# The last query block's norm and transposes as small steps inside the next scans or the last filter stage, and the start values of y inside the attention

## The chip, the cores and the metric

The kernel runs on one core of one Trainium2 chip. Its engines each work through their own queue in order: TensorE (PE; its weight loads are PEld), VectorE (DVE), ScalarE (ACT), GpSimd (POOL) and SyncE, whose queue (SPq) issues the transfers that matter here. The metric is the device time of one execution in microseconds (us); smaller is better.

## The reference

All data are float32. The input `x` has four images of 48 by 48 positions with 128 channels; the kernel treats them one after the other (b = 0 to 3), with L = 2304 positions (tokens) each. Two layers are computed.

```python
# layer 0: group norm, then a state-space block
x = x + _L0_conv_ref(_gn(x), ...)      # projection, 3x3 depthwise convolution, 4 directional scans:
    # h = h * exp(dt * A) + (dt * u) * B;  y = sum over states of h * C;  y += Ds * u
    # norm of y, gate by silu(z), projection back to 128 channels
# layer 1: attention, then a spectral filter block ("STU")
t = _to_tokens(x)
t = t + _L1_attn_ref(_ln_t(t))         # softmax(x x^T) x over all 2304 tokens, x normed per token
t = t + _L1_ffn_ref(_ln_t(t), ...)     # per-token norm to u; causal convolutions of u with 16 filters,
    # with u and with sign-alternating u, each followed by a 128x128 matrix; plus u at 3 lags
```

What this case concerns is `_ln_t(t)` between the attention and the STU: each of the 2304 tokens loses its mean over 128 channels and is divided by the root of its variance plus 1e-5. The result u is needed in two layouts, tokens by channels and (transposed) channels by tokens.

## The kernel before, in words

**Stages.** For each image there is first a scan stage (`scans`, L554), in which the scans of image b are woven with the STU of image b - 1 (`stu`, L957), and for image 0 with a preparation of matrices (`mixture`). Then comes an attention stage: `epilogue(b)` and `attention(b)` woven with `prologue(b + 1)` and `begin_scans(b + 1)`. After image 3 its STU runs alone (`stu_alone`, L1195). So there are four places where an attention stage ends: three times into a scan stage, once into the STU that runs alone. There is no planner: the order of the instructions of every engine is the order in which the generators of L1211 to L1265 emit them. Tile pools opened and closed with the stages set the buffers: a tile of a new stage waits for the last use of whatever lay in its memory.

**Scans.** The 24 chunks of an image (4 directions by 6 pieces of 384 positions) give 192 units of 8 per chunk. For one unit, DVE or POOL multiplies dt*u by the row of B (L481), ACT makes four decays exp(dt*A) (L490), DVE runs four scans (L497), POOL multiplies by C (L506), PE sums over states into y (L514), and DVE adds y to `ya` every fourth unit (L526). The decays and the copied rows of B (L473) lie in a `Ring` (L319) of four PSUM banks (five for image 0), whose first instruction is a DVE memset (L325). Other work may borrow a bank: `mm_hold` takes one, `mm_tile` gives its tile, `mm_done` returns it. `more` (called four times in every step of `scans`) advances the STU beside them.

**STU.** A matmul of filter rows (`tt`, fetched at L1010) with u and with `us`, the sums of two u's (L1051); evictions by ACT (L1067 to L1075); a matrix `G` (L1021) applied at L1114. The output rows are treated in five blocks of up to 126 rows; only the fourth and fifth block read `u[:, 3]`. At the start of each block `begin` fetches the transposed u from DRAM (`ud`, L1082 and L1083).

**Attention and its tail.** Queries are treated in five pieces in the order 0, 4, 1, 2, 3. For every piece 18 slots each make scores (L774), their exponential (L776) and the product with the values (L767). After a piece, `tail(b, J, ...)` (L910) does in steps, one per slot: copy the product (L917), transpose (L921), divide and add to T (L924 to L932), store T to `td` in DRAM (L934), read it back in another token order (`tu`, L937), norm it with `normed` (L149 to L158, with one square on ACT, L152, and one power on POOL, L156), form `us` (L943), transpose on PE (L947), copy to SBUF (L950), store to `ud` (L952). The tails of pieces 0, 4, 1 and 2 run beside the slots of later pieces. Piece 3 is the last, so L785 to L787 run its whole tail when no slot is left.

**Start values of y.** `start_y` (L305) writes Ds*u to `ya` (L309, two DVE instructions). It is called when `begin_scans` has given its last piece, which is at the last slot of the attention, ahead of the tail of piece 3 on DVE.

Of the kernel before, what the change touches and what calls it, by code (L numbers as in the profile page):

```python
# [8 lines left out]
F32 = mybir.dt.float32  # L9
# [6 lines left out]
P = 128  # L16
# [39 lines left out]
def hybrid_kernel(ctx: ExitStack, tc: tile.TileContext, a: dict, out: bass.AP):  # L56
# [262 lines left out]
    class Ring:  # L319


        def __init__(self, pool, n, name):
            self.t = [pool.tile([P, 512], F32, tag=f"ring{i}", name=f"{name}_{i}") for i in range(n)]
            for t in self.t:
                nc.vector.memset(t[:, 0:CS + 2:CS + 1], 0.0)  # L325
            self.free = list(range(n))
            self.held = []

        def take(self):
            return self.free.pop(0)  # L330
# [17 lines left out]
    def mm_done():  # L348
        if isinstance(bank["mm"], Ring):
            bank["mm"].free.append(bank["mm"].held.pop(0))  # L350

    class Chunk:

# [12 lines left out]
        def prep(self, pool):  # L366

            k, name, xc = self.k, self.name, xcs[self.b]
            xdd_ = xdd[k % 2][self.lo // CS]

            def rest(n=1):

                yield
                yield 0
                yield
                for i in range(3 * n - 3):  # L380
                    yield 0 if i % 3 == 1 else None

            if k >= 2:
                xd = self.xd = pool.xd.tile([P, CS], F32, tag="xd", name=f"xd{name}")
                nc.sync.dma_start(xd, xdd_)
            yield from rest(2)
            if k < 2:
                mm_hold()
            yield
            if k < 2:  # L390
                xd = self.xd = pool.xd.tile([P, CS], F32, tag="xd", name=f"xd{name}")
                ps = mm_tile(f"xp{name}")
                for h in range(NH):
                    nc.tensor.matmul(ps[:, :CS], xw[:, h, k, :], in_order(xc[h], k, self.lo, CS),
                                     start=(h == 0), stop=(h == NH - 1))
            yield 2 * CS if k < 2 else 0
            yield
            if k < 2:
                nc.scalar.activation(xd, ps[:, :CS], AF.Identity, bias=onerow)
                mm_done()  # L400
            yield from rest()

            re = pool.one.tile([P, NH, 2, CS], F32, tag="re", name=f"re{name}")
            for h in range(NH):
                mm_hold()
                yield
                ps = mm_tile(f"dt{name}_{h}")
# [4 lines left out]
                mm_done()  # L412
# [36 lines left out]
            yield 0  # L449
            load(1)  # L450
            yield
# [99 lines left out]
            next(preps[2])  # L551
        yield chunks, preps

    def scans(b, chunks, preps, front, sp, back, ring, work, work_cols):  # L554
# [60 lines left out]
        for s in range(len(units) + 2):  # L615
            real = s < len(units)
            enter(s)
            prepare(s)
            if real:
                scan(s, 0)  # L620
            more((s + 0.25) / len(units))
            if 1 <= s <= len(units):
                units[s - 1].times_c()
            if real:
                scan(s, 1)
            if pending:
                pending.pop().add_y()
            prepare(s)
            more((s + 0.5) / len(units))
            spread(s + 2)  # L630
            if real:
                scan(s, 2)
            more((s + 0.75) / len(units))
            prepare(s)
# [9 lines left out]
            more((s + 1) / len(units))  # L644
        for u in pending:
            u.add_y()
        assert next(work, None) is None
# [101 lines left out]
    def attention(b, T, xn, xnT, pool, tmp, ps):  # L749

        pieces = [0, 4, 1, 2, 3]
        slots = [(J, i) for J in pieces for i in range(NT)]
        es, po, tails = [], {}, []  # L760

        def values():
            J, i, e = es.pop(0)
            w = P * PIECES[J]
            if i == 0:
                po[J] = ps.two.tile([P, 512], F32, tag="o", name=f"o{b}_{J}")
            nc.tensor.matmul(po[J][:, :w], xn[:, i], e[:, :w], start=(i == 0), stop=(i == NT - 1))  # L767
# [139 lines left out]
        for t in us[b]:  # L907
            nc.gpsimd.memset(t[KP[-1]:, NM - 1], 0.0)

    def tail(b, J, T, po, pool, ps):  # L910


        u, sums = us[b]
# [18 lines left out]
        nc.vector.tensor_tensor(T[:, :, C - 1], T[:, :, C - 1], s, ALU.subtract)  # L932
        yield
        nc.sync.dma_start(tokens(td, J), T)  # L934
        yield
        x = pool.one.tile([P, 4, C], F32, tag="tu", name=f"tu{b}_{J}")
        nc.sync.dma_start(x[:k], td[512 * J:512 * J + 4 * k].rearrange("(p j) c -> p j c", j=4))  # L937
# [273 lines left out]
    for b in range(B):  # L1211
# [2 lines left out]
        ring = bank["mm"] = Ring(ps.psa, 4 if b else 5, f"ring{b}")  # L1214
        if b == 0:
            mixed = Stage(tc, "m", "right", two=(2, SB))
            scans(b, *first, front, sp, ps, ring, mixture(mixed, ps), MIX_COLS)
# [102 lines left out]
```

## Time and profile before

The median of three runs is 5857.22 us (5853.99 to 5860.59).

| what | value |
|---|---|
| profiled execution, its own time | 5857.79 us |
| its span | 5856.1 us |
| busy share of the span: PE, DVE, ACT, POOL | 84%, 73%, 57%, 62% |
| scan stages | about 110 to 1090, 1361 to 2382, 2643 to 3665, 3934 to 4932 us |
| STU alone | about 5171 us to the end |
| DVE scans L497 | 3072 instructions, 2702.4 us |
| PE filter matmuls L1051 | 818.0 + 811.8 + 797.0 us in the three largest groups |

The span is what the profile covers; the 1.7 us between it and the execution's own time lie before and after it. Busy shares are averages over stages with different limits, so the places where stages meet have to be read in the timeline, which lists the instructions of all engines in order of time: start, duration, engine, line, operation, tiles, and in square brackets how long the engine had been idle and which work ended that. Durations of PE are modelled.

### The profile page before, as it was taken

How to read it: one execution, taken by the hardware profiler on the slowest of the kernel's cores; microseconds unless marked ns; L12 is line 12 of the kernel's file. 1: busy time of each engine (PE TensorE's matmuls, PEld its weight loads, DVE VectorE, ACT ScalarE, POOL GpSimd, SP SyncE). 2: the span in 40 equal slices, each digit the busy share in tenths (PEclk: the TensorE clock that was granted, in tenths of full speed). 3: DMA queues.
4: the chain of work that ended last, by engine and by line, in shares of the span. 5: the costliest groups of instructions: out<-in, count | busy, mean ns of one | idle time of the engine just before them, and what ended most of it. 6: DMA issues, size and time to landing. Idle time of an engine off the chain costs nothing. (4 is left out here: it accounts for less than half of the span.)

```text
span 5856.1 us, 74080 instructions
## 1 busy us (share of the span) xinstructions
PE 4937.2 (84%) x23922; PEld 3149.3 (54%) x23922; DVE 4267.9 (73%) x4883; ACT 3333.3 (57%) x6957; POOL 3622.6 (62%) x1823
## 2 busy tenths in 40 slices
PE   3566555697999998788999998779999998889999
PEld 1211111344666667445566666436566666468889
DVE  6999999657999998548999997548999997200000
ACT  2777777346777776247777775247777764332111
POOL 1999999505889998207889997108898986000000
PEclk6777787798999999899999999889999999999999
DMA  3444454116878777127777787027877775045546
GB/s 107 162 161 162 160 168 158 56 48 190 240 250 258 249 254 265 43 70 216 231 252 251 250 266 240 21 89 223 243 251 257 248 261 188 14 116 158 158 146 209
DMA packets 750563, 1066.86 MB, mean 182 GB/s; under 512 B 158528, under 2 KB 561088, under 8 KB 750144
## 3 DMA queue, kind: packets, MB, share of 16 engines
q1 hardware_dynamic: 744352, 1058.83, 57.2%
q10 hardware_dynamic: 5824, 3.30, 0.3%
q8 instruction: 191, 3.13, 0.2%
q14 instruction: 196, 1.61, 0.1%
HBM read 943.80 MB, written 117.98 MB: 181 GB/s over the span
## 5 line engine op out<-in xcount | busy, mean ns | idle before, releaser
L497 DVE TENSOR_TENSOR_SCAN s<-ring,s 128x385 f32<-128x385 f32 x3072 | 2702.4, 938 | 123.3 <-ACT ring L490 121.9
L506 POOL TENSOR_TENSOR s<-s,bc 128x1536 f32<-128x1536 f32 x768 | 2440.0, 3179 | 128.5 <-DVE s L497 73.3
L490 ACT ACTIVATE ring<-rep,A 128x384 f32<-128x384 f32 x3072 | 1759.3, 584 | 778.6 <-DVE s L481 456.8
L481 POOL TENSOR_TENSOR s<-rep,bc 128x1536 f32<-128x1536 f32 x288 | 994.4, 3453 | 131.2 <-DMA bc<-xdd 124.2
L481 DVE TENSOR_TENSOR s<-rep,ring 128x1536 f32<-128x1536 f32 x480 | 831.4, 1733 | 86.6 <-ACT ring L473 36.5
L1051 PE MATMUL cx<-tt,us 128*128 128x254 f32 (+7 forms) x3840 | 818.0, 355 | 74.0 <-ACT U L1075 46.9
L514 PE MATMUL y<-s,csum 128*32 128x384 f32 x6144 | 718.1, 542 | 191.7 <-POOL s L506 119.5
L1051 PE MATMUL cx<-tt,u 128*128 128x254 f32 (+7 forms) x3840 | 811.8, 354 | 67.3 <-ACT cy L1067 67.2
L1051 PE MATMUL cy<-tt,u 128*128 128x252 f32 (+5 forms) x3840 | 797.0, 351 | 30.3 <-DMA tt<-fd 30.3
L1051 PEld LDWEIGHTS cx<-tt,u 128*128 128x128 f32 x3840 | 644.8, 192 | 312.6 <-issue 113.3
L1051 PEld LDWEIGHTS cx<-tt,us 128*128 128x128 f32 x3840 | 645.3, 193 | 275.2 <-issue 91.2
L1051 PEld LDWEIGHTS cy<-tt,u 128*128 128x128 f32 x3840 | 648.9, 193 | 178.0 <-issue 117.9
L1114 PE MATMUL pr<-U,G 128*128 128x288 f32 (+6 forms) x2048 | 590.5, 420 | 15.4 <-DMA G<-gd 15.1
L1141 DVE TENSOR_TENSOR res<-res,ot 126x512 f32<-126x512 f32 (+1 forms) x20 | 13.4, 672 | 686.8 <-PE ot L1135 686.8
L1114 PEld LDWEIGHTS pr<-U,G 128*128 128x128 f32 x2048 | 340.6, 191 | 169.4 <-issue 96.2
L514 PEld LDWEIGHTS y<-s,csum 128*32 128x32 f32 x6144 | 126.8, 112 | 551.0 <-issue 283.2
L776 ACT ACTIVATE e<-s,shift 128x512 f32<-128x512 f32 (+1 forms) x360 | 231.1, 644 | 328.5 <-PE s L774 327.9
L156 POOL TENSOR_TENSOR ln_vu<-ln_vu,mhalf 128x4 f32<-128x4 f32 (+1 forms) x20 | 21.8, 1092 | 625.5 <-DVE ln_vu L155 625.5
L774 PE MATMUL s<-xnT 128*128 128x512 f32 (+1 forms) x720 | 355.2, 578 | 45.7 <-ACT xnT L736 23.3
L894 PE MATMUL G<-M,W 128*128 128x256 f32 (+3 forms) x512 | 233.2, 571 | 189.1 <-ACT W L884 80.3
L767 PE MATMUL o<-e,xn 128*128 128x512 f32 (+1 forms) x720 | 341.6, 557 | 4.5 <-ACT e L776 4.5
L1074 ACT COPY U<-cx 128x252 f32<-128x252 f32 (+1 forms) x320 | 111.6, 349 | 400.8 <-PE cx L1051 398.4
(170 smaller groups left out, 4110.7 us busy)
## 6 DMA issues: line engine op xcount, KB each, us to landing
rep<-dtdud SPq DMA_DIRECT2D x768, 384.0 KB
bc<-xdd SPq DMA_DIRECT2D x3072, 48.0 KB
tt<-fd SPq DMA_DIRECT2D x192, 577.0 KB
tt<-fd SPq DMA_DIRECT2D x192, 505.0 KB
dtdud<-re SPq DMA_DIRECT2D x192, 384.0 KB
tt<-fd SPq DMA_DIRECT2D x192, 379.0 KB
G<-gd SPq DMA_DIRECT2D x192, 256.0 KB
tt<-fd SPq DMA_DIRECT2D x64, 506.0 KB
```

What stands on the lines that cost most here:

```text
L481: eng.tensor_tensor(s, self.ch.rep[self.h][:, :, 1], bt.unsqueeze(1).to_broadcast([P, G4, CS]), ALU.mult)
L490: nc.scalar.activation(ring.body(self.dA[g]), ch.rep[self.h][:, g, 0], AF.Exp, scale=A[:, ch.k, self.h * G4 + g, self.q:self.q + 1])
L497: nc.vector.tensor_tensor_scan(s, ring.decays(i, ch.rev), s, 0.0, ALU.mult, ALU.add)
L506: nc.gpsimd.tensor_tensor(self.s, self.s, ch.bc[Q4 + self.q].unsqueeze(1).to_broadcast([P, G4, CS]), ALU.mult)
L514: nc.tensor.matmul(ch.y[g * DL:(g + 1) * DL, :CS], csum, self.s[:, g], start=(self.q == 0), stop=(self.q == Q4 - 1))
L767: nc.tensor.matmul(po[J][:, :w], xn[:, i], e[:, :w], start=(i == 0), stop=(i == NT - 1))
L774: nc.tensor.matmul(p[:, :w], xnT[:, i * P:(i + 1) * P], xnT[:, 512 * J:512 * J + w], start=True, stop=True)
L776: nc.scalar.activation(e[:, :w], p[:, :w], AF.Exp, bias=shift)
L894: nc.tensor.matmul(p[:, :n], W[:, q if t else 0, i], M[t][:, i].unsqueeze(1).to_broadcast([P, n, C]), start=(t == 0 and i == 0), stop=(t = ...
L1051: nc.tensor.matmul(p4[:, 1:3, v - (hi - at):] if g else p4[:, 0:4:3, v - (hi - at):], x, t[:, :, hi - 1 - at + J * P:end if end >= 0 else ...
L1074: nc.scalar.copy(U[n][:, 2:8:5], p[:, :4 * (w + 1)].rearrange("p (e m) -> p e m", e=4)[:, 0:4:3, 1:])
L1114: nc.tensor.matmul(o if q else o.rearrange("p f r m -> p r f m"), G, U[n][:, 4 * q:4 * q + 4, v0:v1].rearrange("p (a b) m -> p a b m", a=2 ...
```

## The change

Three things change.

1. The tail of the last piece (J = 3) returns after storing T to `td` (L934). The read back, the norm, the sums, the transposes and the store to `ud` move to a new generator `finish(b)`, which the scan stage of the next image advances four times in every step, and which the STU that runs alone advances once at each of its yields. The norm is written with other instructions: `bn_stats` and `bn_aggr` on DVE instead of two reductions, a subtraction, a square and a product; the power and one small product on POOL; the scaling by four ACT instructions; the sums `us` by two PE matmuls with the identity, copied by ACT. Its PSUM comes from the ring, of which it borrows one bank at a time, twice. The STU that runs alone gets a ring of two banks for it. The small tiles `fin`, `fst` and `fmv` are new in the pool `keep`.
2. `start_y(b + 1)` is called before `begin_scans(b + 1)`, 25 slots before the attention's end instead of at its last slot.
3. `mm_hold` returns the bank that it took, and `mm_tile` and `mm_done` are given it, so that two borrowers can hold banks at the same time. For `prep` this leaves the order as it was.

```diff
@@ Ring, mm_hold, mm_tile, mm_done
     def mm_hold():
-        if isinstance(bank["mm"], Ring):
-            bank["mm"].held.append(bank["mm"].take())
-
-    def mm_tile(name):
-        if isinstance(bank["mm"], Ring):
-            return bank["mm"].body(bank["mm"].held[0])
+        return bank["mm"].take() if isinstance(bank["mm"], Ring) else None
+
+    def mm_tile(name, hold=None):
+        if hold is not None:
+            return bank["mm"].body(hold)
...
@@ scans: next(finish, None) behind each of the four more(...) of a step
             more((s + 0.25) / len(units))
+            next(finish, None)
...
@@ attention
-                tails.append(tail(b, J, T, po.pop(J), tmp, ps))
+                tails.append(tail(b, J, T, po.pop(J), tmp, ps, J == pieces[-1]))
@@ new
+    LAST = 3
+
+    def finish(b):
+        u, sums = us[b]
+        x = keep.tile([P, 4, C], F32, tag="fin", name=f"fin{b}")
+        st = keep.tile([P, 4, 6], F32, tag="fst", name=f"fst{b}")
+        mv = keep.tile([P, 4, 4], F32, tag="fmv", name=f"fmv{b}")
+        yield
+        nc.sync.dma_start(x, td[512 * LAST:512 * LAST + 4 * P].rearrange("(p j) c -> p j c", j=4))
+        for i in range(7):
+            yield
+        for j in range(4):
+            nc.vector.bn_stats(st[:, j], x[:, j])
+        for j in range(4):
+            nc.vector.bn_aggr(mv[:, j, 0:2], st[:, j:j + 1])
+        nc.vector.tensor_scalar_add(mv[:, :, 1], mv[:, :, 1], 1e-5)
+        nc.vector.tensor_scalar_mul(mv[:, :, 0], mv[:, :, 0], -1.0)
+        yield
+        nc.gpsimd.tensor_tensor(mv[:, :, 2], mv[:, :, 1], mhalf[:, :4], ALU.pow)
+        nc.gpsimd.tensor_tensor(mv[:, :, 3], mv[:, :, 0], mv[:, :, 2], ALU.mult)
+        for i in range(7):
+            yield
+        for j in range(4):
+            nc.scalar.activation(u[:, LAST, j], x[:, j], AF.Identity, bias=mv[:, j, 3:4], scale=mv[:, j, 2:3])
+        for i in range(4):
+            yield
+        for n in range(2):
+            hold = mm_hold()
+            p = mm_tile(f"fin{b}_{n}", hold)
+            for i, j in enumerate(range(4)[3 * n:3 * n + 3]):
+                nc.tensor.transpose(p[:, i * P:(i + 1) * P], u[:, LAST, j], ident)
+            if n:
+                for i in range(2):
+                    nc.tensor.matmul(p[:, P:3 * P], ident, u[:, LAST, 2 * i:2 * i + 2].rearrange("p j c -> p (j c)"),
+                                     start=(i == 0), stop=(i == 1))
+            yield
+            yield
+            if n:
+                nc.scalar.copy(x[:, 3], p[:, :P])
+                nc.scalar.copy(sums[:, LAST].rearrange("p j c -> p (j c)"), p[:, P:3 * P])
+            else:
+                nc.scalar.copy(x[:, :3].rearrange("p j c -> p (j c)"), p[:, :3 * P])
+            mm_done(hold)
+            yield
+            yield
+        nc.sync.dma_start(ud[:, :, 1 + P * LAST:1 + P * (LAST + 1)], x)
@@ tail
         nc.sync.dma_start(tokens(td, J), T)
+        if last:
+            return
         yield
@@ the stages
-            scans(b, *first, front, sp, ps, ring, stu_alone(b - 1, ps, 1), STU_COLS)
+            scans(b, *first, front, sp, ps, ring, finish(b - 1), stu_alone(b - 1, ps, 1), STU_COLS)
...
             front = Stage(tc, f"f{b + 1}", "left", one=(1, SB), xd=(3, SB), rep=(3, SB))
+            start_y(b + 1)
             pieces = begin_scans(b + 1, front)
...
-                if first:
-                    start_y(b + 1)
...
-    ps = Stage(tc, "end", "right", psc=(2, PSUM), psp=(1, PSUM))
+    ps = Stage(tc, "end", "right", psa=(1, PSUM), psc=(2, PSUM), psp=(1, PSUM))
+    bank["mm"] = Ring(ps.psa, 2, "ringe")
+    end = finish(B - 1)
     for _ in stu_alone(B - 1, ps, 2):
+        next(end, None)
+    for _ in end:
         pass
```

More of the change, by code (lines that the diff above doesn't have):

```diff
@@ L326, in __init__ @@
             self.free = list(range(n))
-            self.held = []
         def take(self):
@@ L338, in mm_hold, with mm_done @@
     def mm_hold():
-        if isinstance(bank["mm"], Ring):
-            bank["mm"].held.append(bank["mm"].take())
-    def mm_tile(name):
-        if isinstance(bank["mm"], Ring):
-            return bank["mm"].body(bank["mm"].held[0])
+        return bank["mm"].take() if isinstance(bank["mm"], Ring) else None
+    def mm_tile(name, hold=None):
+        if hold is not None:
+            return bank["mm"].body(hold)
         pool, tag = bank["mm"]
         return pool.tile([P, 512], F32, tag=tag, name=name)
-    def mm_done():
-        if isinstance(bank["mm"], Ring):
-            bank["mm"].free.append(bank["mm"].held.pop(0))
+    def mm_done(hold):
+        if hold is not None:
+            bank["mm"].free.append(hold)
     class Chunk:
@@ L387, in prep @@
             if k < 2:
-                mm_hold()
+                hold = mm_hold()
             yield
@@ L391, in prep @@
                 xd = self.xd = pool.xd.tile([P, CS], F32, tag="xd", name=f"xd{name}")
-                ps = mm_tile(f"xp{name}")
+                ps = mm_tile(f"xp{name}", hold)
                 for h in range(NH):
@@ L399, in prep @@
                 nc.scalar.activation(xd, ps[:, :CS], AF.Identity, bias=onerow)
-                mm_done()
+                mm_done(hold)
             yield from rest()
@@ L404, in prep @@
             for h in range(NH):
-                mm_hold()
+                hold = mm_hold()
                 yield
-                ps = mm_tile(f"dt{name}_{h}")
+                ps = mm_tile(f"dt{name}_{h}", hold)
                 nc.tensor.matmul(ps[:, :CS], dtw[:, k, h * P:(h + 1) * P], xd, start=True, stop=True)
@@ L411, in prep @@
                 nc.scalar.copy(re[:, h, 0], ps[:, :CS])
-                mm_done()
+                mm_done(hold)
                 if h == 0:
@@ L552, in begin_scans, with scans @@
         yield chunks, preps
-    def scans(b, chunks, preps, front, sp, back, ring, work, work_cols):
+    def scans(b, chunks, preps, front, sp, back, ring, finish, work, work_cols):
         units = [Unit(ch, h, q) for ch in chunks for h, q in quads]
@@ L629, in scans @@
             more((s + 0.5) / len(units))
+            next(finish, None)
             spread(s + 2)
@@ L633, in scans @@
             more((s + 0.75) / len(units))
+            next(finish, None)
             prepare(s)
@@ L644, in scans @@
             more((s + 1) / len(units))
+            next(finish, None)
         for u in pending:
@@ L908, in begin_stu, with tail @@
             nc.gpsimd.memset(t[KP[-1]:, NM - 1], 0.0)
-    def tail(b, J, T, po, pool, ps):
+    LAST = 3
[24 more added lines that the diff above has]
+        for n in range(2):
+            hold = mm_hold()
+            p = mm_tile(f"fin{b}_{n}", hold)
[12 more added lines that the diff above has]
+                nc.scalar.copy(x[:, :3].rearrange("p j c -> p (j c)"), p[:, :3 * P])
+            mm_done(hold)
+            yield
+            yield
+        nc.sync.dma_start(ud[:, :, 1 + P * LAST:1 + P * (LAST + 1)], x)
+    def tail(b, J, T, po, pool, ps, last):
         u, sums = us[b]
@@ L1216, in hybrid_kernel @@
             mixed = Stage(tc, "m", "right", two=(2, SB))
-            scans(b, *first, front, sp, ps, ring, mixture(mixed, ps), MIX_COLS)
+            scans(b, *first, front, sp, ps, ring, iter(()), mixture(mixed, ps), MIX_COLS)
             mixed.close()
         else:
-            scans(b, *first, front, sp, ps, ring, stu_alone(b - 1, ps, 1), STU_COLS)
+            scans(b, *first, front, sp, ps, ring, finish(b - 1), stu_alone(b - 1, ps, 1), STU_COLS)
         ps.close()
```

## The prediction

> **What bounds the kernel now.** I first read the busy time of each engine stage by stage. The columns are the stretch, then busy time and (instructions) of PE, PEld, DVE, ACT, POOL, then PE's clock and the DMA share.
>
> ```profile
> 1335.00:1361.00 26.00, 7.62 (x20) 3.25 (x18) 13.28 (x25) 6.21 (x9) 4.39 (x2) 0.64 0.18 57
> ...
> 1461.00:2380.00 919.00, 860.22 (x4818) 581.77 (x4818) 855.14 (x918) 636.62 (x1365) 808.71 (x391) 0.98 0.78 248
> ...
> 5155.00:5178.00 23.00, 5.65 (x15) 2.38 (x13) 6.39 (x17) 1.22 (x2) 1.01 (x1) 0.57 0.26 62
> ```
>
> Inside a scan stage DVE (93%) and PE (94%) set the pace together. Between the stages there are holes of over 20 us in which every engine is at half load or less. There are four. What fills such a hole is read in the timeline (start, duration, engine, line, operation); this is the one before the fourth scan stage:
>
> ```profile
> 3912.18 2.74 DVE L309 TENSOR_SCALAR ya<-xc,dsum 128x2304 f32<-128x2304 f32 x2
> ...
> 3914.84 0.68 DVE L917 COPY oT<-o 128x512 f32<-128x512 f32 x1
> ...
> 3918.72 0.16 DVE L932 TENSOR_TENSOR T<-T,den 128x4 f32<-128x4 f32 x1
> 3918.90 0.38 SPq L934 DMA_DIRECT2D td<-T  x1
> 3921.21 0.33 SPq L937 DMA_DIRECT2D tu<-td  x1
> 3923.85 0.69 DVE L149 TENSOR_REDUCE ln_su<-tu 128x4 f32<-128x512 f32 x1 [4.97 <-DMA tu<-td]
> ...
> 3928.24 3.90 DVE L158 TENSOR_TENSOR u<-u,ln_vu 128x512 f32<-128x512 f32 x1 [1.19 <-POOL ln_vu L156]
> ...
> 3934.02 0.56 SPq L952 DMA_DIRECT2D ud<-uT  x1
> 3934.07 0.09 DVE L325 MEMSET ring<- 128x2 f32 x4 [1.47 <-ACT uT L950]
> ...
> 3934.68 4.64 SPq L1010 DMA_DIRECT2D tt<-fd  x4
> ...
> 3938.01 3.50 DVE L497 TENSOR_TENSOR_SCAN s<-ring,s 128x385 f32<-128x385 f32 x4
> ...
> 3941.09 1.34 PEld L1051 LDWEIGHTS cx<-tt,us 128*128 128x128 f32 x4 [7.59 <-DMA tt<-fd]
> ```
>
> The tail of the last piece runs here alone, step after step. From the last write of T (end 3918.88) to the ring's memset (3934.07) are 15.19 us: two transfers and the norm, transposes and copy behind them. Scans and filter matmuls both stand behind it: the memset waits for ACT's L950 (it takes over that PSUM), and the fetch of tt stands behind L952 in SP's queue. The two earlier places have 15.18 and 15.15 us. At the last place there is no scan, only the STU:
>
> ```profile
> 5159.01 0.16 DVE L932 TENSOR_TENSOR T<-T,den 128x4 f32<-128x4 f32 x1
> ...
> 5171.61 4.89 SPq L1010 DMA_DIRECT2D tt<-fd  x4
> ...
> 5177.94 1.34 PEld L1051 LDWEIGHTS cx<-tt,us 128*128 128x128 f32 x4 [5.71 <-DMA tt<-fd]
> ```
>
> [...] L158 above took 3.90 us beside a POOL multiply of 3.42 us (L481), and 0.69 us elsewhere. This matters for work moved into a stage where POOL is 88% busy. [...] The trace has 2.31 us from L934 to L937, which waits for it, and 2.64 us from L937 to L149; so 5 us of each hole are transfers that more engine speed couldn't shorten, only other work could hide.
>
> **What is taken off the path.** After L932 the ring's memset has nothing left to wait for: in the changed program it follows L932 on DVE directly. Gain 15.17 us at each of three places. tt is issued right behind L934, its first tile without waiting for that store, the second only after the store landed (+2.3 us); the first filter matmul needs only the first tile. It came 6.4 us after its issue before, so it too moves by about 15 us: SP is not late next. The inputs of the first units (rep, bc) have landed by 1343 us at the first place, where the DMA share falls to 0, ahead of the new start near 1345. At the last place tt moves from 5171.61 to about 5159.75 (0.58 us behind L932, as there are L934's 0.36 us and the waits around it): 11.86 us.
>
> **start_y moved.** L309's 2.74 us stood ahead of L917, but PE's last product ended only about 0.4 us before L917 began. Gain 0.4 us. At its new place it stands behind L275 and ahead of L158 of piece 1's tail. At the first place L275 ends at 1287.82; plus 2.74 and 0.69 for L158 gives 1291.25, while PE reached the transposes L947 at 1290.66. PE waits about 0.65 us there, and in the attention PE is the pace. So this part is worth -0.25 us per place, about nothing. If DVE didn't stand in PE's way it would be +0.4, if the wait also cost PE's next exponential, some -1.5.
>
> **What the moved steps cost inside a scan stage.**
> - DVE: four `bn_stats` over 128. The nearest row is L200, 0.560 us over 384. [...] Four `bn_aggr` of 6 values: L202 took 0.318 us on 36, so an estimate of 0.2, four 0.8. Two small tensor_scalar at 0.17 (L155): 0.34. Sum 2.3 us.
> - [...] Bounds: 0, and one POOL multiply (3.18 us, L506) each. L438, two-source work in the same stage, has a mean of 0.957 us against 0.515 us without POOL. I take 0.7 us together.
> - `bn_stats` waits for fin<-td, and the next scans stand behind it on DVE. By SP's order fin is issued about 10.8 us after the memset, behind four tt (381 KB each), two ux, mue, res and one dtdud; with fin about 3.2 MB. Before, 2.1 MB had moved 11.6 us after the memset, at some 250 GB/s at the end; 1.1 MB more are 4.3 us[...]: landed near +18.5. DVE gets there after the ninth scan: the scans of the second unit began at 1374.90, five more at 0.88 make 1379.3, +18.9 us. A tie; I take 0.5 us (0 to 4).
> - POOL: a power at 1.01 (L156) and a product of at most that, 2.0 us, where POOL waited 17.4 us for DVE in 87 us of the stage's start: hidden; if not, 2 us. ACT: four scalings at 0.31 (L97's shape) and copies of 384, 128 and 256 at 0.48, 0.28, 0.37: 2.4 us on an engine 69% busy, with decays behind it. PE: four transposes at 0.15 and two 256-wide products at 0.25, 1.1 us. The borrowed bank leaves three for the decays, twice for about half a step. ACT and bank together: 0.5 us (0 to 4).
>
> Sum 4.0 us. Net per scan stage 15.17 - 0.25 - 4.0 = 10.9; three give 32.8 us.
>
> **In the STU that runs alone** DVE and POOL are idle, so the norm is free there; ACT reaches the scalings in the third item, some 20 us behind L932, with fin landed at about 13. PE does 1.1 us more on the path, and 0.4 us for copies between its evictions: 11.86 - 1.5 = 10.4 us. [...]
>
> **Sum.** 32.8 + 10.4 = 43.2 us. Against the profiled execution, 5857.8 - 43.2 = 5814.6; it stands 0.6 us above the median of 5857.2, so 5814 us.
>
> **Rivals.**
> - The moved steps are wholly hidden (PE, ACT and DVE all have waits in the stage's start, where DVE is 85% busy), and the first tt lands sooner for going alone: 3 x 15.4 + 13 = 59 us, 5798 us. Against it: after the start DVE is 93% busy with few gaps.
> - The steps hurt more: [...] fin is 3 us late, bank and ACT cost 3: 15 us per stage instead of 4. That is 33 us less gain in all, 5847 us; half of it gives 5830.
> - On the other side, slower: fin lands so late that `bn_stats` stops DVE longer than the hole it replaced. Place: DVE's queue after the ninth scan. Price: each us late is one us of every scan stage. It decides from 18 us late on, landing beyond +37 us: 3 x (15 - 4 - 18) + 10 = -11 us. At 20 us late it is slower by 17 us, 5874 us. For it: the start of the stage is at 250 to 340 GB/s. Against it: only 3.2 MB are ahead, and res<-td, issued just before, was part of the same rush that ended in 12 to 17 us.
> - The change doesn't do what it says: scans wait at once for something else, such as tt by ACT's L1067, which stands ahead of the third unit's L473 (DVE waited 5.4 us there). It waits already and moves with tt, so this takes 1 or 2 us at most: inside the range.
>
> **Numbers.** My forecast as summed, within 12 us on either side: 0.62. Hidden: 0.13. Hurting more, still faster: 0.18. So small a gain that it can't be told (0.2% or 11.7 us is about what a measurement here can tell): 0.04. Slower: 0.03. The range goes from the hidden case's 5797 to 5834 in the hurting one.
>
> **What would show it.** Right: the memset L325 within 0.3 us of L932 at three places; tt's first issue 0.6 us behind L932; no L149 to L158 of the fourth piece; the scan stages no more than 5 us longer than before from memset to last scan. Wrong: a long DVE wait on fin, tensor_scalar of 2 us or more, ACT waiting for POOL ahead of the scalings, or PE waiting at L947 in the attention for more than a us.

## The result, and the profile after

The changed kernel took 5810.67 us in the median of four runs (5808.85 to 5815.86), the kernel before beside it 5855.60 us. The ratio is 0.9925, 95% interval 0.9908 to 0.9942. The forecast was 5814 us, a gain of 43.2 us. A second measurement on another occasion (e9 below) gave 5805.58 us against 5852.36 us, ratio 0.9922 (0.9910 to 0.9935). The mean of the two gains is 45.9 us. The profiled execution took 5808.85 us (before: 5857.79), its span 5807.1 us, so 49.0 us of span are to be found.

Line numbers shift. What was L932 and L934 (last write of T, store to `td`) is now L983 and L985; tt is fetched at L1063 (L1010), the filter matmuls are L1104 (L1051), their first eviction L1120 (L1067); in the scans L479, L488, L495, L504 stand for L481, L490, L497, L506.

**The stretches.** Busy time of the changed kernel in the stretches that were shown of before, in the same columns; the third starts where the last attention ends now.

```profile
1335.00:1361.00 26.00, 16.20 (x37) 8.43 (x36) 11.86 (x23) 11.79 (x22) 6.78 (x3) 0.69 0.58 150
...
1461.00:2380.00 919.00, 859.05 (x4787) 580.58 (x4785) 853.51 (x915) 631.54 (x1352) 805.54 (x390) 0.98 0.78 246
5117.00:5140.00 23.00, 14.02 (x46) 9.77 (x46) 4.33 (x22) 4.33 (x9) 0.18 (x1) 0.78 0.68 173
```

In the first stretch PE is busy for 16.2 us where it had 7.6, and the DMA engines for 58% where they had 18%. The long stretch in the middle of the stage is what it was: DVE and PE at 93% both. The change acts at the edges: the moved steps run in the first 51 us of a stage (in the first one the memset is at 1347.7 us, the store to `ud` at 1398.4 us).

**The third place and the fourth**, before the last scan stage and before the STU that runs alone, in the timeline of the changed kernel:

```profile
3894.72 0.15 DVE L983 TENSOR_TENSOR T<-T,den 128x4 f32<-128x4 f32 x1
3894.88 0.09 DVE L325 MEMSET ring<- 128x2 f32 x4
3894.90 0.38 SPq L985 DMA_DIRECT2D td<-T  x1
...
3895.37 3.98 SPq L1063 DMA_DIRECT2D tt<-fd  x4
...
3898.82 3.50 DVE L495 TENSOR_TENSOR_SCAN s<-ring,s 128x385 f32<-128x385 f32 x4
...
3900.72 1.34 PEld L1104 LDWEIGHTS cx<-tt,us 128*128 128x128 f32 x4 [8.00 <-DMA tt<-fd]
...
3904.18 0.42 SPq L922 DMA_DIRECT2D fin<-td  x1
...
5120.90 0.15 DVE L983 TENSOR_TENSOR T<-T,den 128x4 f32<-128x4 f32 x1
...
5121.54 4.69 SPq L1063 DMA_DIRECT2D tt<-fd  x4
...
5127.32 1.34 PEld L1104 LDWEIGHTS cx<-tt,us 128*128 128x128 f32 x4 [7.66 <-DMA tt<-fd]
```

The memset stands 0.01 us behind the last write of T; it stood 15.19 us behind. From 5120.90 on it is the fourth place. There the first filter matmul starts 6.27 us behind the last write of T, where it was 18.77 us.

**Where the 49.0 us are.** From such timelines I read for both kernels the end of the last write of T, the ring's memset, and the end of the stage's last scan:

| part of the span | before | after | gain, us |
|---|---|---|---|
| last write of T to memset, three places | 15.19, 15.16, 15.19 | 0.01, 0.00, 0.01 | 45.5 |
| memset to last scan, three stages | 995.8, 1006.5, 1003.0 | 1004.8, 1001.3, 1004.0 | -4.8 |
| last write of T to the end of the span | 696.9 | 686.1 | 10.9 |
| all ahead of the first such place | 1345.2 | 1347.7 | -2.5 |
| between last scan and last write of T, three times | | | -0.1 |

The second row warns: a single stage differs by up to 9 us from one profile to the next. e1 below runs the scan stages of the kernel before, and has 1002.7, 997.6 and 1003.7 where that kernel itself has 995.8, 1006.5 and 1003.0; the sums agree within 1.3 us. The changed kernel's second profile (e9) has 1000.4, 1005.5 and 1000.9, a mean of 1002.3 us where 1003 had been expected, and a sum 3.3 us below that of its first profile. So what the moved steps cost inside a stage can't be read from one stage of one profile; that is what most of the experiments are for. In the new kernel's scan stage the steps themselves look like this (timeline, DVE and then POOL at the first place):

```profile
1367.05 0.85 DVE L926 BATCH_NORM_STATS2 fst<-fin 128x6 f32<-128x128 f32 x4
1367.81 0.37 DVE L928 BATCH_NORM_AGGREGATE fmv<-fst 128x2 f32<-128x6 f32 x4
1368.21 1.60 DVE L929 TENSOR_SCALAR fmv<-fmv 128x4 f32<-128x4 f32 x1
1369.72 0.16 DVE L930 TENSOR_SCALAR fmv<-fmv 128x4 f32<-128x4 f32 x1
...
1366.61 3.17 POOL L504 TENSOR_TENSOR s<-s,bc 128x1536 f32<-128x1536 f32 x1
1369.89 1.01 POOL L932 TENSOR_TENSOR fmv<-fmv,mhalf 128x4 f32<-128x4 f32 x1
```

DVE is kept from its scans from 1367.05 to 1369.79, 2.74 us. No bracket stands behind L926: DVE didn't wait for `fin`. Of the 2.74 us, 1.60 go to L929, an addition to four values per partition, which ends as POOL's multiply L504 does (1369.78). The same holds at the other two places and in e9's profile: 1.60 or 1.61 us each time, ending with the multiply. The statistics ran beside that multiply at the pace that they had without it in the last stage (four `bn_stats` in 0.85 and 0.87 us, four `bn_aggr` in 0.37 and 0.36 us).

### The profile page after: what moved, and what is told of

Same layout as the page of the kernel before. It is cut to its first block, busy times and chain, and to the rows that moved or that the text cites. A ratio compares the mean times of both kernels' runs of the same rounds, so it can differ in the third digit from the quotient of the medians.

```text
span 5807.1 us, 74156 instructions
## 1 busy us (share of the span) xinstructions
PE 4940.5 (85%) x23938; PEld 3150.9 (54%) x23938; DVE 4254.5 (73%) x4897; ACT 3338.6 (57%) x6977; POOL 3624.8 (62%) x1827
## 3 DMA queue, kind: packets, MB, share of 16 engines
q14 instruction: 196, 1.61, 0.1%
## 5 line engine op out<-in xcount | busy, mean ns | idle before, releaser
L495 DVE TENSOR_TENSOR_SCAN s<-ring,s 128x385 f32<-128x385 f32 x3072 | 2700.4, 937 | 128.8 <-ACT ring L488 127.6
L504 POOL TENSOR_TENSOR s<-s,bc 128x1536 f32<-128x1536 f32 x768 | 2440.0, 3179 | 128.7 <-DVE s L495 66.9
L488 ACT ACTIVATE ring<-rep,A 128x384 f32<-128x384 f32 x3072 | 1758.5, 583 | 788.1 <-DVE s L479 458.4
L479 POOL TENSOR_TENSOR s<-rep,bc 128x1536 f32<-128x1536 f32 x288 | 994.5, 3453 | 153.7 <-DMA bc<-xdd 149.0
L479 DVE TENSOR_TENSOR s<-rep,ring 128x1536 f32<-128x1536 f32 x480 | 830.9, 1732 | 87.6 <-issue 39.4
L1104 PE MATMUL cx<-tt,us 128*128 128x254 f32 (+7 forms) x3840 | 817.9, 355 | 90.6 <-ACT U L1128 58.4
L1104 PE MATMUL cx<-tt,u 128*128 128x254 f32 (+7 forms) x3840 | 812.0, 354 | 64.4 <-ACT cy L1120 64.3
L1104 PE MATMUL cy<-tt,u 128*128 128x252 f32 (+5 forms) x3840 | 792.4, 349 | 27.7 <-DMA tt<-fd 27.6
L1104 PEld LDWEIGHTS cx<-tt,u 128*128 128x128 f32 x3840 | 644.7, 192 | 309.7 <-issue 113.7
L1104 PEld LDWEIGHTS cx<-tt,us 128*128 128x128 f32 x3840 | 644.4, 192 | 287.7 <-issue 89.8
L1104 PEld LDWEIGHTS cy<-tt,u 128*128 128x128 f32 x3840 | 643.5, 191 | 176.4 <-issue 111.3
L156 POOL TENSOR_TENSOR ln_vu<-ln_vu,mhalf 128x4 f32<-128x4 f32 (+1 forms) x16 | 19.3, 1208 | 515.3 <-DVE ln_vu L155 480.4
L1127 ACT COPY U<-cx 128x252 f32<-128x252 f32 (+1 forms) x320 | 111.5, 349 | 394.0 <-PE cx L1104 393.5
```

The costliest lines, as they stand in the source:

```text
L479: eng.tensor_tensor(s, self.ch.rep[self.h][:, :, 1], bt.unsqueeze(1).to_broadcast([P, G4, CS]), ALU.mult)
L488: nc.scalar.activation(ring.body(self.dA[g]), ch.rep[self.h][:, g, 0], AF.Exp, scale=A[:, ch.k, self.h * G4 + g, self.q:self.q + 1])
L495: nc.vector.tensor_tensor_scan(s, ring.decays(i, ch.rev), s, 0.0, ALU.mult, ALU.add)
L504: nc.gpsimd.tensor_tensor(self.s, self.s, ch.bc[Q4 + self.q].unsqueeze(1).to_broadcast([P, G4, CS]), ALU.mult)
L1104: nc.tensor.matmul(p4[:, 1:3, v - (hi - at):] if g else p4[:, 0:4:3, v - (hi - at):], x, t[:, :, hi - 1 - at + J * P:end if end >= 0 else ...
L1127: nc.scalar.copy(U[n][:, 2:8:5], p[:, :4 * (w + 1)].rearrange("p (e m) -> p e m", e=4)[:, 0:4:3, 1:])
```

## The experiments

Each ratio is to the kernel before, run on the same chip beside it; "us gained" is the difference of the two medians. The changed kernel gains 45.9 us.

| run | edit to the changed kernel | ratio (95%) | us gained |
|---|---|---|---|
| e1 | only the last place changed | 0.9981 (0.9974 to 0.9988) | 11.3 |
| e2 | only the three scan places changed | 0.9946 (0.9932 to 0.9961) | 32.7 |
| e3 | moved steps left out | 0.9910 (0.9893 to 0.9926) | 55.5 |
| e4 | moved steps five times | 0.9978 (0.9971 to 0.9986) | 14.1 |
| e5 | statistics right behind the load's issue | 0.9951 (0.9936 to 0.9965) | 29.0 |
| e6 | `start_y` at its old place | 0.9923 (0.9899 to 0.9946) | 46.0 |
| e7 | two small DVE operations on POOL | 0.9911 (0.9896 to 0.9925) | 51.8 |
| e8 | STU given out later in the first step | 0.9925 (0.9909 to 0.9942) | 44.9 |
| e9 | none | 0.9922 (0.9910 to 0.9935) | 46.8 |
| e10 | as e7, timed again | 0.9899 (0.9884 to 0.9914) | 57.6 |
| e11 | STU given out later in two steps | 0.9947 (0.9933 to 0.9960) | 32.1 |
| e12 | e4 and e10 together | 0.9934 (0.9920 to 0.9947) | 38.0 |

**The theory** is that of the prediction: three holes and a late last STU are taken off the path, and the moved steps cost a few us per scan stage. **The rivals:** the steps are hidden; they cost much more; a late `fin` stops DVE us for us.

### e1 and e2: the two kinds of place alone

In e1 the whole tail of the last piece stays in the attention for images 0 to 2, in e2 for image 3.

```diff
-  tails.append(tail(b, J, T, po.pop(J), tmp, ps, J == pieces[-1]))
+  tails.append(tail(b, J, T, po.pop(J), tmp, ps, b in (3,) and J == pieces[-1]))   # e1; e2: (0, 1, 2)
...
-  ring, finish(b - 1), stu
+  ring, finish(b - 1) if b - 1 in (3,) else iter(()), stu
```

> The change kept only at the end: image 3 is finished inside the STU that runs alone, images 0 to 2 have their whole tail in the attention as before; start_y stays at its new place. Theory (the hole behind the attention is the gain, place by place): about 10 us faster than before, ratio 0.998; the holes before the three scan stages stay at 15.2 us. Rival (the gain is that of the later start values of y, or of the new memory layout): about the whole 45 us stay, ratio 0.9925.

> The counterpart: images 0 to 2 are finished inside the scan stages, image 3 has its whole tail as before. Theory: about 34 us faster than before, ratio 0.994; tt's first issue in the last stage is 12.4 us behind the last write of T again. The two parts of the gain add up to that of the changed kernel within the measurement.

Measured: 11.3 us (7 to 15 by the interval) and 32.7 us (23 to 40); the prediction had 10.4 and 32.8. e1 keeps the new place of `start_y` and the new memory layout and has lost most of the gain, so its rival falls. The two parts add up to 44.0 us, the whole change has 45.9: nothing shows that they help or hinder each other. In e1's profile the holes of 15.2 us are back (1344.46 to 1359.63, and so on), and the last stage takes 684.9 us.

The three holes are 45.5 us wide, and e2 gains 32.7: some 12.8 us, or 4.3 us per scan stage, are lost again inside the stages. Worked out from the whole change less e1 (45.9 - 11.3 = 34.6), it is 3.6 us.

### e3 and e4: what the moved steps cost

e3 leaves the steps out, with their load and store, and puts zeros in place of that piece of u; only its time is of use. e4 has norm, scalings, transposes, sums and copies five times in each scan stage (load and store once).

```diff
-  ring, finish(b - 1), stu
+  ring, iter(()), stu                                   # e3, and no finish beside the last STU
...
+  for again in reversed(range(5 if b < B - 1 else 1)):  # e4, around all between load and store
```

> The changed kernel without the moved steps: load, norm, sums, transposes and store of the fourth piece are left out, u and ud of that piece are zeros written elsewhere. Theory (the steps cost about 4 us in each scan stage and 1.5 us at the end): 13.5 us faster than the changed kernel, ratio to before about 0.990. Rival (they are hidden by other waits in the scan stages): within 3 us of the changed kernel, ratio 0.9925. If the lengths of the scan stages differ from the changed kernel's by several us in both directions, their scatter isn't made by the steps.

> The changed kernel with the steps from the statistics to the PSUM copies done five times over in each scan stage (the first four times the transposed copies go back into PSUM; the result is the same). Theory at 4 us per stage and time: 4 x 3 x 4 = 48 us slower than the changed kernel, no gain over before is left. At the 1.6 us per stage that the mean of the three stages of the changed kernel shows: 19 us slower. Rival (hidden): no more than 5 us slower.

e3 is 9.6 us better than the changed kernel, where 13.5 us had been expected; some 1.7 us of it belong to the last stage (684.1 against 685.8 us, the mean of the changed kernel's two profiles). That leaves 2.6 us per scan stage, with wide margins. In e4 twelve repetitions cost 45.9 - 14.1 = 31.8 us, 2.65 us each. That is below the 4.0 us of the sum and far above nothing: the steps are not hidden. With e1 and e2, four ways of measuring give 2.6, 2.65, 3.6 and 4.3 us. Profiles give a lower figure: from memset to last scan the three stages sum up to 3005.3 and 3004.0 us with the old stages (before, e1), and to 3010.1, 3006.8, 3006.4 and 3015.6 us with the new ones (changed kernel, e9, e6, e2). That is 5 us more in the mean, 1.7 us per stage, from single executions up to 9 us apart. Like the 3.6 and 4.3 us of e1 and e2, it has the steps' cost less what an earlier tt gives back inside the stage.

The groups of e4's profile with the tile `fmv` (minimum, median and maximum of one, in ns) show which term is not a constant. e4 has one line more, so its L930 is L929 of the changed kernel:

```profile
L929 DVE BATCH_NORM_AGGREGATE fmv<-fst x64: 144/148/168, 1366.3 to 5181.1; 128x2 f32<-128x6 f32 x64
L930 DVE TENSOR_SCALAR fmv<-fmv x16: 171/800/2630, 1366.7 to 5181.3; 128x4 f32<-128x4 f32 x16
L931 DVE TENSOR_SCALAR fmv<-fmv x16: 156/158/165, 1368.2 to 5181.4; 128x4 f32<-128x4 f32 x16
L933 POOL TENSOR_TENSOR fmv<-fmv,mhalf x16: 1008/1010/1319, 1368.4 to 5181.6; 128x4 f32<-128x4 f32 x16
```

The same operation on four values takes 0.17 us or up to 2.63 us, by where it falls in a POOL multiply. The longest and a short one in e4's timeline:

```profile
1445.07 0.17 DVE L930 TENSOR_SCALAR fmv<-fmv 128x4 f32<-128x4 f32 x1
...
4096.56 3.18 POOL L504 TENSOR_TENSOR s<-s,bc 128x1536 f32<-128x1536 f32 x1
4097.14 2.63 DVE L930 TENSOR_SCALAR fmv<-fmv 128x4 f32<-128x4 f32 x1
```

Of the 15 in the scan stages, 12 meet a POOL multiply, and each of the 12 ends within 0.03 us of that multiply's end; the other three take 0.17 us. The twelve added ones take 0.80 us in the mean, the first of each stage 1.61 us. If the held time counts in full, an estimate for the single steps is 2.65 + 0.8 = 3.4 us.

### e7, e9, e10, e12: the operation that is held

e7 and e10 are one kernel: the two small DVE operations become two POOL products with constants, ahead of the power. e9 is the changed kernel beside e10, and e12 the five repetitions with the same edit.

```diff
-  nc.vector.tensor_scalar_add(mv[:, :, 1], mv[:, :, 1], 1e-5)
-  nc.vector.tensor_scalar_mul(mv[:, :, 0], mv[:, :, 0], -1.0)
   yield
+  nc.gpsimd.tensor_tensor(mv[:, :, 1], mv[:, :, 1], cst[:, 0:4], ALU.add)   # 1e-5
+  nc.gpsimd.tensor_tensor(mv[:, :, 0], mv[:, :, 0], cst[:, 4:8], ALU.mult)  # -1
```

> The changed kernel with the two small tensor_scalar of the norm moved from DVE to two POOL products with constants. In the changed kernel the first of them takes 1.60 us in each scan stage and ends with POOL's multiply. Theory (DVE sets the pace, so the held time is on the path): 1.6 us less per stage, 5 us faster than the changed kernel, ratio about 0.9917. Rival (PE paces, or the held time is caught up): no difference.

> The changed kernel as it is, beside the runs below on the same chip: a ratio of 0.9925 to the kernel before, as in its first measurement. Its three scan stages, from the ring's memset to the last scan, are again 1003 us in the mean, and one by one differ from the first profile's by up to 5 us either way.

> The two small DVE operations on fmv as two products of 0.2 us on POOL, as in the earlier run of this edit, with more rounds. Theory that what DVE is held there (1.60 us in each scan stage) reaches the end: 3 x 1.6 = 4.8 us faster than the changed kernel beside it, a ratio lower by 0.0008. Rival, that DVE's later waits take it up: no difference, and the 5 to 8 us seen earlier were scatter.

> The norm, transposes, sums and copies five times in each scan stage, as in the earlier run of that edit, and now with the two small DVE operations as products on POOL, all five times. 12 repetitions stand above the single ones. Theory that what the moved steps cost is mostly DVE held at the first small operation (0.17 to 2.6 us there, 0.8 in the median): the price of one repetition falls from 2.6 to about 1.2 us, so 14 us above the same edit with single steps (ratio 0.9899), which is a ratio of 0.992. Rival, that the price is in the work itself, on DVE (1.7 us), ACT (3.1 us) and PE (1.1 us) and in the bank: 2.6 us again, 31 us, 0.995.

e7 alone decided nothing. Timed again, e10 took 5794.78 us (5789.91 to 5795.69) beside e9's 5805.58 us (5802.37 to 5815.91): the ranges don't meet, and the edit is worth 10.8 us there, 5.9 us by e7, where 4.8 were expected. e10 is the fastest kernel of this study. Its gain (57.6 us) is even above that of e3, which has none of the moved steps (55.5 us), so one of these two is off by some us, and 10.8 us may be too high. On POOL the two take 0.20 us each:

```profile
L933 POOL TENSOR_TENSOR fmv<-fmv,cst x4: 200/204/207, 1367.7 to 5126.0; 128x4 f32<-128x4 f32 x4
L934 POOL TENSOR_TENSOR fmv<-fmv,cst x4: 199/201/207, 1367.8 to 5126.2; 128x4 f32<-128x4 f32 x4
L935 POOL TENSOR_TENSOR fmv<-fmv,mhalf x4: 1002/1004/1012, 1368.0 to 5126.3; 128x4 f32<-128x4 f32 x4
```

e12 takes the size from many repetitions. It gains 38.0 us where e4 gains 14.1, and their intervals don't meet. The single version gains 51.8 (e7) or 57.6 us (e10), so one repetition costs 1.2 to 1.6 us, where it cost 2.65 us. The theory said 1.2, the rival 2.6: 1.0 to 1.5 us of the price, about half, go with the two small operations, their held time included. In e4 DVE spends 0.9 us on the two in an added repetition. The remaining 1.2 to 1.6 us are near what DVE's statistics need (0.85 + 0.37 = 1.2 us in the timeline above); how much of it is ACT's or the borrowed bank's was not told apart.

### e5: what a wait for `fin` costs

```diff
-  for i in range(7):
+  for i in range(1 if b < B - 1 else 7):
       yield
   for j in range(4):
       nc.vector.bn_stats(st[:, j], x[:, j])
```

> The changed kernel with the statistics one step behind the issue of the load in the scan stages instead of seven steps (the last stage as changed). This is the slower rival made true in part: DVE comes to the statistics some 7 us behind the memset, and fin lands near 18. Theory (each us that fin is late is a us of the stage, less the wait of about 5 us that DVE has there anyway): a DVE wait of 8 to 12 us on fin, 6 to 9 us per stage, 18 to 27 us slower than the changed kernel, ratio to before about 0.9965. Rival (the stage takes the wait up later): no more than 5 us slower than the changed kernel.

It loses 16.9 us against the changed kernel, 5.6 us per stage, a little less than the 6 to 9 expected. Its timeline at the first place:

```profile
1346.26 0.09 DVE L325 MEMSET ring<- 128x2 f32 x4
...
1362.87 0.87 DVE L926 BATCH_NORM_STATS2 fst<-fin 128x6 f32<-128x128 f32 x4 [10.01 <-DMA fin<-td]
1363.65 0.36 DVE L928 BATCH_NORM_AGGREGATE fmv<-fst 128x2 f32<-128x6 f32 x4
1364.05 0.17 DVE L929 TENSOR_SCALAR fmv<-fmv 128x4 f32<-128x4 f32 x1
```

`fin` lands 16.6 us behind the memset, and DVE stood for 10.0 us (10.2 and 9.7 us at the other places). Why is that only 5.6 us of time? The waits of DVE in the first 100 us of this stage, summed by what ended them; first the changed kernel:

```profile
DVE s L495 <- ACT ring L488: 8.4, 5, 2.5
DVE s L479 <- ACT ring L471: 5.3, 2, 4.8
DVE s L479 <- issue: 3.1, 2, 2.0
DVE s L479 <- POOL s L504: 1.5, 1, 1.5
```

then e5:

```profile
DVE fst L926 <- DMA fin<-td: 10.0, 1, 10.0
DVE s L495 <- ACT ring L488: 9.7, 11, 2.3
DVE s L479 <- POOL s L504: 1.6, 1, 1.6
DVE s L479 <- issue: 1.2, 2, 0.9
DVE s L479 <- ACT ring L471: 0.7, 2, 0.5
DVE s L479 <- POOL carry L503: 0.4, 1, 0.4
```

18.3 us of waits against 23.6 us: 5.3 more. The new wait of 10.0 us takes the place of the one for L471 (5.3 to 0.7 us), which was coming anyway. One thing makes e5 look cheaper than the wait is: its L929 meets no POOL multiply and takes 0.17 us, in all three stages, where the changed kernel pays 1.60 us. If those 1.4 us count in full, the wait itself costs about 7 us per stage (an estimate). The theory of one us per us, less the wait of about 5 us that was there anyway, gives 5 us for a wait of 10. Only one length of wait was measured, so the price of each further us stays open.

### e8 and e11: can the other wait be had?

That wait of 4.8 us for L471 is ACT standing behind its evictions L1120 to L1128, which wait for the first filter matmuls (3.72 us ahead of L1120 and 1.55 us ahead of L1127; L471 follows at 1359.44 us). Two edits give the STU's first items out later, so that L471 comes ahead of L1120 on ACT.

```diff
-  more((s + 0.25) / len(units))
+  if b and s == 0:                    # e8: one item, and none at the second call of this step
+      done[0] += next(work)
+  else:
+      more((s + 0.25) / len(units))
...
+  if s > 1 or not b:                  # e11: one item, and then none at any call of two steps
       more((s + ...) / len(units))
```

> The changed kernel with only the first matmul of the STU emitted in the first half of the first step of a scan stage, so that ACT copies the third unit's row of B ahead of the STU's first eviction, which waits for tt. In the changed kernel DVE waits about 4.8 us for that copy. Theory (DVE sets the pace from its first scan on): that wait goes, 3 to 4 us less per stage, 9 to 12 us faster than the changed kernel, ratio about 0.9907. Rival (PE's filter matmuls set the pace, and they start with tt at the same time): no difference, and DVE waits as long somewhere in the next two steps.

> In the first two scan steps of each scan stage, only the first of the STU's matmul items is given out, and the items catch up from the third step on. Theory that the scans set the pace at the start of the stage and lose the 4.8 us there in which DVE waits for ACT, which waits for PE: up to 5 us faster per stage, 15 us, a ratio of 0.990. Rival, that PE sets the pace over the stage and every item put off there is missing later: no difference or slower by what PE stands idle, up to 10 us per stage, a ratio of 0.9976.

In e8 the time doesn't move (44.9 us gained against 45.9), and the wait is nearly as long, elsewhere. Timeline at its first place:

```profile
1352.78 1.73 DVE L479 TENSOR_TENSOR s<-rep,ring 128x1536 f32<-128x1536 f32 x1
1354.43 0.95 DVE L495 TENSOR_TENSOR_SCAN s<-ring,s 128x385 f32<-128x385 f32 x1
1359.71 0.96 DVE L495 TENSOR_TENSOR_SCAN s<-ring,s 128x385 f32<-128x385 f32 x1 [4.33 <-ACT ring L488]
```

The third multiply L479 now runs at once, and the second scan behind it waits 4.33 us instead. e11 puts the STU off further and is slower by 13.8 us than the changed kernel (14.7 us beside e9). Its waits of DVE in the first 100 us of the first scan stage after an attention, then those of PE:

```profile
DVE s L495 <- ACT ring L488: 9.7, 6, 2.5
DVE s L479 <- ACT ring L471: 3.9, 2, 3.4
DVE fst L932 <- DMA fin<-td: 3.0, 1, 3.0
DVE s L479 <- issue: 2.2, 2, 2.0
DVE s L479 <- POOL s L504: 1.5, 1, 1.5
...
PE cx L1110 <- ACT cy L1126: 5.2, 3, 3.1
```

DVE gets ahead, then waits 3.0 us for `fin` and 3.4 us for L471 two units later: 20.3 us of waits where there were 18.3. PE waits 5.2 us for ACT's eviction L1126, where the changed kernel has 2.8 us for the same one (L1120). Neither edit won the wait back. Why e11 is slower stays open: filter items put off, as its rival has it, and the new wait for `fin` (3.0, 3.2 and 2.2 us in the three stages), which the edit brought with it, were not told apart.

### e6: `start_y` back at its old place

```diff
-  start_y(b + 1)
   pieces = begin_scans(b + 1, front)
...
+  if first:
+      start_y(b + 1)
```

> The changed kernel with the start values of y at their old place, at the last slot of the attention. Theory: no difference that can be measured (0.25 us per place in favour of the old one); in the trace the copy of the last product begins right behind the start values, the hole is no longer than in the changed kernel by more than 0.5 us, and PE doesn't wait at the transposes of piece 1. Rival (the earlier place is part of the gain): the attention ends about 2.7 us later at each of three places, 8 us slower.

No difference: 46.0 us gained; the interval of this run is wide, so I go by the trace. The attention with its epilogue, from the epilogue's first matmul to the last write of T, takes 264.4, 264.4 and 264.2 us in e6, 264.6, 266.5 and 265.0 us in the changed kernel, 264.2, 266.9 and 264.5 us in the one before. e6's timeline at the end of the first attention, DVE alone:

```profile
1338.23 1.02 DVE L436 TENSOR_TENSOR re<-re,xc 128x384 f32<-128x384 f32 x2 [12.12 <-ACT re L418]
1339.17 2.74 DVE L309 TENSOR_SCALAR ya<-xc,dsum 128x2304 f32<-128x2304 f32 x2
1341.83 0.68 DVE L968 COPY oT<-o 128x512 f32<-128x512 f32 x1
```

The changed kernel's timeline has the same copy 3.19 us behind L436 instead of 3.60, since there it waits only for PE's product:

```profile
1340.65 1.03 DVE L436 TENSOR_TENSOR re<-re,xc 128x384 f32<-128x384 f32 x2 [11.51 <-ACT re L418]
...
1343.84 0.69 DVE L968 COPY oT<-o 128x512 f32<-128x512 f32 x1 [2.16 <-PE o L769]
```

## Why the prediction was right, step by step

The forecast gain of 43.2 us came as 44.9 and 46.8 us, by the way that was forecast: the holes are gone and the steps cost less than the holes were wide.

**The holes.** Forecast 15.17 us at three places; 15.16 to 15.19 us were there, and no more than 0.01 us is left. SP was not late next, as said: the first filter matmul stands 6.3, 5.6 and 5.8 us behind the memset, where it stood about 7.0. "The first tt lands sooner for going alone" was put into a rival; it does land sooner, by about 1 us, but the reason given was not tested.

**The last STU.** Forecast 11.86 - 1.5 = 10.4 us; 10.9 by the profiles, 11.3 by e1. The start moved by 12.5 us (18.77 to 6.27), 0.6 us more than the issue of tt did by the forecast, as tt landed sooner here too; 1.6 us were given back later. No part is owed to the clock: the four filter matmuls at the start took 2.05 us after and 2.06 us before, at a granted clock of 0.50 both times. The norm had DVE and POOL to itself there, as forecast: in 672 us of that stage of the kernel before, DVE was busy for 2.75 us and POOL not at all.

**`start_y`.** Forecast 0.4 us gained at the copy and 0.65 us lost on PE; the trace has 0.41 us gained at the first place (e6 against the changed kernel), and a PE wait of 0.15 us for L158 (0.98 us on its weight load). Whatever is left lies under the scatter of the attention's length, as forecast.

**The steps inside a scan stage.** Forecast 4.0 us; the experiments say 2.6 to 4.3 us, the profiles 1.7 us. This term decided the forecast, and its parts were off both ways: for DVE's statistics and small operations about 2.0 and 1.04 us had been set down, and the first place has 1.16 and 1.58 us. That the sums agree (3.0 and 2.7 us) is luck in part.

- DVE's statistics. `bn_stats` took 0.276 us, `bn_aggr` 0.150 us (forecast 0.2). Four in a row took 0.85 and 0.37 us, less than four times one, as one begins before the one ahead has ended (the first `bn_aggr` at 1367.81, the last `bn_stats` until 1367.89). For the four `bn_stats` the prediction's 2.3 us for DVE leave about 1.2 us beside the 0.8 and 0.34 us, my estimate for 128 elements: the kernel before shows `bn_stats` over 384 only (0.560 us).
- The small operations. 0.34 us were set down for the pair, and 0.7 us for the time that they stand beside POOL's work; 1.60 + 0.16 us came. The first ended with POOL's multiply in each of the three stages, the second never: POOL's next work, L932, waits for it (the multiply ends at 1369.78, L932 starts at 1369.89). The bound of "one POOL multiply each" was one too many. Why the addition ends with the multiply was not shown; `bn_stats` and `bn_aggr` ran beside the same multiply at their own pace (0.85 and 0.37 us for four).
- `fin`. Forecast to land at +18.5 us (11.6 + 4.3 make 15.9; the rest was my estimate), with DVE there at +18.9, "a tie", 0.5 us. It landed at +16.3 to +16.8 us by e5, DVE came at +17.7 to +19.3, and nothing was paid.
- ACT. The scalings took 0.485 us each, not 0.31: the row that was taken as the nearest (L97, 0.309 us for 128 elements) has not the same operands. With the copies (0.485, 0.269 and 0.38 us) ACT does 3.1 us, not 2.4. How much of that comes on top of the scans, with the borrowed bank, was put at 0.5 us and was not measured.
- POOL did 1.01 + 0.21 us, not 2.0.

**The signs.** Those of being right came true but one: the scan stages were to be no more than 5 us longer, and they are 9.0 us longer, 5.2 us shorter and 1.0 us longer in the two profiles, which is within what e1 shows for stages with the same instructions. Of the signs of being wrong, the 1.60 us of L929 and PE's 0.98 us come near their bounds of 2 and 1 us; ACT waited for POOL ahead of the scalings in the last stage alone (2.4 us).

**The rivals.** "Wholly hidden" (5798 us) falls by e4: 2.65 us per repetition. "Hurts more" (15 us per stage, 6.4 us of it for two small operations of one POOL multiply's length each) falls by all four measures. "Slower" had the right place and too high a price: a wait of 10.0 us for `fin` cost 5.6 us, or about 7 us with the held operation reckoned in (e5), so such a wait would probably decide later than at 18 us, and `fin` was not late at all. That scans would wait at once for something else came true as set down, 4.8 us at L471 where 5.4 us were before, and e8 and e11 did not win it by giving the filter work out later.

## What to carry to other kernels

A tail that runs alone between two stages is worth its whole width before costs (three times 15.2 us here), read from the timeline as the stretch from its last needed write to the next stage's first instruction; what it costs when woven into a full stage is a sum of small pieces, here about the time that it took on VectorE, one of the two busiest engines (2.7 us; the experiments gave 2.6 to 4.3 us). A tiny VectorE operation beside long GpSimd multiplies need not be tiny: here it took 1.60 us instead of 0.17 us, and was better on GpSimd (0.20 us), whose next instruction needed it. A new wait early in a stage cost here only what the waits already there didn't take up (10.0 us of wait for `fin` in e5, 5.3 us more waits in the first 100 us), so sum the waits of the stretch before and after rather than adding the new one.

## What the runs showed of the hardware

- An addition of a constant to 128x4 values on VectorE took 0.17 us where no GpSimd multiply ran, 1.60 us in all three scan stages, and up to 2.63 us in e4, ending each time with GpSimd's multiply of 128x1536; the same sum on GpSimd took 0.20 us in e10, where it began at 1367.7 us in the first stage, 1.6 us behind the end of VectorE's statistics (1366.09).
- A ScalarE scaling with scale and bias per partition took 0.485 us for 128 elements, where a plain copy of 128 took 0.269 us.
- Scan stages with the same instructions differ by up to 9 us out of 1000 between profiles (1006.5 and 997.6 us for the same second stage), while the sums over three stages differ by 1.3 us (before, e1) and 3.3 us (changed kernel, e9). What sets the single stage's length was not found.
- e10's gain of 5.9 to 10.8 us over the changed kernel is more than the 5.3 us that DVE had spent on the two operations (3 x 1.76). e12 gains 23.9 us over e4, 1.6 us for each of fifteen repetitions, where DVE had spent about 1.05 us on the two. Whether the rest is scatter stays open.
